# Expert tiles that are full whatever the last block of tokens chooses are listed before that block is routed

## The chip, the cores and the metric

The program runs on one core of one Trainium2 chip. The metric is the device time of one execution in microseconds (us), taken as a median of several runs. A core has five engines with a queue each: TensorE (PE in the profile; PEld is its loading of weights), VectorE (DVE), ScalarE (ACT), GpSimd (POOL) and SyncE (SP), which here issues most transfers (DMA). Instructions of an engine go in the order of its queue and wait on semaphores for what other engines make. All numbers are 32-bit floats.

## The reference

An image of 256 channels and 64 x 64 places passes four layers. Layers 0 and 1 are convolutions and layer 2 is an attention with a mixture of experts (hidden width 256); they come before the change. Layer 3, where the change lies, works on 4096 tokens of 256 channels:

```python
t = t + _L3_attn_ref(_ln_t(t), ...)      # one head: softmax(Q K^T / 16) V over all 4096 tokens
t = t + _L3_ffn_ref(_ln_t(t), ...)       # eight experts, two for each token

gate_logits = xf @ Wg + bg
top_w, top_i = jax.lax.top_k(gate_logits, 2)
top_w = jax.nn.softmax(top_w, axis=-1)
for e in range(8):
    h = jax.nn.gelu(xf @ W1[e] + b1[e])              # 256 -> 1024
    out = out + w_dense[:, e:e + 1] * (h @ W2[e] + b2[e])   # 1024 -> 256
```

So each token goes to two of eight experts, and which two is known only when its attention is done, normalized and multiplied by Wg.

## The kernel before

**Attention** (attn3, L2385 to L2668). The tokens stand in SBUF as `t`, 32 tiles of 128 rows. Queries are taken in eight blocks of 512 (NBLK = 8, NB = 512), and for each block the keys in 16 pairs of tiles (NPAIR = 16). One step of the loop is `scores(g)` for one pair (L2541), `values(g - 2)` for the pair two before (L2575) and `fetch(g + 3)`, which loads keys (L2514). At the end of a block VectorE puts the four accumulators together into oT (L2535 to L2537). In the pairs of the next block come `finish` (L2595), one per tile of the finished block: a product of oT with the value weights (recorded in the helper L148), a division and an addition into `t`, and then `route`, a generator of five steps: statistics and norm; two turns (transposes, L2061) through PSUM; logits, the two best experts, their weights and counts (`top`, `exp`, `weigh`, `count`); and last `place`, `find` and `scatter`, which puts each row of the block by eight indirect DMAs of POOL (L2113) into `xs`, a DRAM array with room of 4096 rows for each expert. A row carries its number, its two weights and its first expert beside its 256 channels (CX = 260). A step of the route is taken every second pair. PE's and POOL's instructions stand in written order in this loop (`tc.manual_schedule`); a scheduler orders the other engines.

At the start of attention, `add(b)` (L2434) adds the results of layer 2's experts to `t`: two loads of `ys`, one issued by SP and one by ACT (L2332), into one of two buffers `room`, which `route` uses too, and two additions (L2440).

After the last block, finish and route of that block follow at once, with nothing else to do for PE, and then **tile_table** (L2121): from the counts per expert it makes a table of 39 tiles of 256 rows (NTILE = 39): expert and first row of each (`tab`), and for the last rows of an expert which are in use (`in`, `off`). Then attention's pools are released.

**Experts** (experts L2173, expert_tiles L2190). 36 tiles always run (MOST = 36), three more only if the table uses them. A tile: `load` reads the expert and the row out of the table into registers of SP and issues loads of x (256 rows), w1 and w2; `turn` transposes x by four PE instructions and a copy by VectorE into xT (L2222); `first` is 32 products into f_h_ps with eight gelus of ACT (L2232); `where` works out on VectorE to which rows of `ys` the results go; `sides` makes sums of weights on POOL (wt, L2259); `second` is 56 products into f_ya_ps and f_yb_ps, additions on VectorE, scaling on ACT (L2301) and two indirect DMAs of POOL (L2302). The loads run two tiles ahead, from three buffers of w1 and w2; the loop (L2314) puts `first(i)` and `turn(i + 1)` ahead of `second(i - 1)`. A scheduler sets the order on the engines here. At last the results are added to `t` and stored (limits3 L2670, store L1361).

Of the kernel before, what the change touches and what calls it, by code (L numbers as in the profile page):

```python
# [19 lines left out]
P = 128  # L20
C = 256
# [28 lines left out]
NI = MT // P  # L50

# [37 lines left out]
class Net:  # L89
# [2031 lines left out]
    def tile_table(self, S, wp, bank):  # L2121


        nc = self.nc
        tl = lambda shape, tag, dt=F32: wp.tile([P] + shape, dt, tag="f_" + tag, name="f_" + tag, bufs=1)
# [8 lines left out]
        nc.vector.tensor_copy(cnt, ci)  # L2134
        ends = tl([NE], "ends")
# [4 lines left out]
        tau = tl([NTILE], "tau")  # L2140
        nc.vector.tensor_scalar(tau, self.count, last, None, ALU.min)
        past = tl([NTILE, NE], "past")
        nc.vector.tensor_tensor(past, bc(ends, 1, NTILE), bc(tau, 2, NE), ALU.is_le)
        ex = S["ex"]
        nc.vector.tensor_reduce(ex, past, AX.X, ALU.add)
        tab = S["tab"]
        nc.vector.tensor_scalar_mul(tab[:, 0, :], ex, float(P))
        nc.vector.tensor_tensor(past, past, bc(cnt, 1, NTILE), ALU.mult)
        skip = tl([NTILE], "skip")
        nc.vector.tensor_reduce(skip, past, AX.X, ALU.add)  # L2150
        nc.vector.tensor_sub(tau, tau, skip)
        nc.vector.tensor_scalar_mul(tau, tau, float(MT))
# [6 lines left out]
        nc.vector.tensor_tensor(past, bc(ex, 2, NE), bc(self.count[:, :NE], 1, NTILE), ALU.is_equal)  # L2159
        nc.vector.tensor_tensor(past, past, bc(rows, 1, NTILE), ALU.mult)  # L2160
        nc.vector.tensor_reduce(skip, past, AX.X, ALU.add)
        nc.vector.tensor_sub(skip, skip, tau)
        nc.vector.tensor_scalar(tau, self.count, last, None, ALU.is_le)
        nc.vector.tensor_mul(skip, skip, tau)

        nc.vector.tensor_tensor(S["in"], bc(self.nth[:, :NI], 1, NTILE), bc(skip, 2, NI), ALU.is_lt)
        nc.vector.tensor_scalar(S["off"], S["in"], -1.0, 1.0, ALU.mult, ALU.add)
        for i in range(0, NTILE, 4):
            n = min(4, NTILE - i)
            part = S["off"][:, i : i + n, :].rearrange("p i k -> p (i k)")  # L2170
            nc.vector.scalar_tensor_tensor(part, self.nth[:, : n * NI], float(2 * N), part, ALU.add, ALU.mult)

    def experts(self, S):  # L2173

        tc = self.tc

        def some(tiles):
            with (
                tc.tile_pool(name=f"f{S['L']}e", bufs=5 if S["L"] == 2 else 3) as wp,
                tc.tile_pool(name=f"f{S['L']}e_ps", bufs=1, space=PSUM) as ps,  # L2180
            ):
                self.expert_tiles(S, tiles, wp, ps)

        some(range(MOST))
        used = self.nc.values_load(S["used"][0:1, 0:1], min_val=0, max_val=NTILE,
                                   skip_runtime_bounds_check_because="worked out from counts of tokens")
        with tc.If(used > MOST):
            some(range(MOST, NTILE))

    def expert_tiles(self, S, tiles, wp, ps):  # L2190
        nc, A = self.nc, self.A
        L, tab = S["L"], S["tab"]
        hidden = 256 if L == 2 else 1024
        KH = hidden // P
        ahead = 3 if L == 2 else 2
        why = "worked out from counts of tokens"

        def load(i):
            e = nc.values_load(tab[0:1, 0, i : i + 1], engines=[mybir.EngineType.SP], min_val=0, max_val=(NE - 1) * P,
                               skip_runtime_bounds_check_because=why)  # L2200
            row = nc.values_load(tab[0:1, 1, i : i + 1], engines=[mybir.EngineType.SP], min_val=0, max_val=NE * N - MT,
                                 skip_runtime_bounds_check_because=why)
            x = wp.tile([P, NI, CX], F32, tag="x", name="f_x", bufs=ahead + 3)
            rows = lambda: nc.sync.dma_start(out=x, in_=self.xs[bass.ds(row, MT), :].rearrange("(i p) c -> p i c", p=P))

            if i > 0:
                rows()
            w1 = wp.tile([P, 2 * hidden + KH], F32, tag="w1", name="f_w1")
            nc.sync.dma_start(out=w1, in_=A[f"f{L}_w1"][bass.ds(e, P), :])
            w2 = wp.tile([P, KH * C + C], F32, tag="w2", name="f_w2")  # L2210
            nc.sync.dma_start(out=w2, in_=A[f"f{L}_w2"][bass.ds(e, P), :])
            if i == 0:
                rows()
            return x, w1, w2

        def turn(x):
            p = ps.tile([P, 2, MT], F32, tag="x", name="f_x_ps", bufs=2)
            for k in range(2):
                for i in range(NI):
                    nc.tensor.transpose(p[:, k, i * P : (i + 1) * P], x[:, i, k * P : (k + 1) * P], self.ident)  # L2220
            xT = wp.tile([P, 2, MT], F32, tag="xT", name="f_xT")
            nc.vector.tensor_copy(xT, p)  # L2222
            return xT

        def first(xT, w1):
            h = wp.tile([P, KH, MT], F32, tag="h", name="f_h")
            for m in range(KH):
                if m % 2 == 0:
                    p = ps.tile([P, 2, MT], F32, tag="h", name="f_h_ps", bufs=3)
                q = p[:, m % 2, :]  # L2230
                self.mm(q, [(w1[:, kt * hidden + m * P : kt * hidden + (m + 1) * P], xT[:, kt, :]) for kt in range(2)])
                nc.scalar.activation(h[:, m, :], q, AF.Gelu, bias=w1[:, 2 * hidden + m : 2 * hidden + m + 1])  # L2232
            return h

        def where(i, x):
# [3 lines left out]
            op = nc.vector  # L2239
            op.tensor_scalar(first, x[:, :, C + 3], S["ex"][:, i : i + 1], None, ALU.is_equal)  # L2240
# [4 lines left out]
            op.tensor_tensor(to, to, S["in"][:, i, :], ALU.mult)  # L2245
            op.tensor_tensor(at, to, S["off"][:, i, :], ALU.add)
# [60 lines left out]
        tiles = list(tiles)  # L2307
# [3 lines left out]
        xT = turn(ld[tiles[0]][0])  # L2311
        to = where(tiles[0], ld[tiles[0]][0])
        done = None
        for i in tiles:  # L2314
# [3 lines left out]
            h = first(xT, w1)  # L2318
            now = (i, h, w2, sides(w2)) + to
            if i < tiles[-1]:  # L2320
                xT = turn(ld[i + 1][0])
                to = where(i + 1, ld[i + 1][0])
            if done is not None:
                second(*done)
            done = now
        second(*done)

    def outputs(self, b, y):

        src = self.ys[: 2 * N, :].rearrange("(r b p i) c -> b p r (i c)", r=2, b=NBLK, i=TPB)  # L2330
        for r in range(2):
            (self.nc.sync, self.nc.scalar)[r].dma_start(out=y[:, r].rearrange("p i c -> p (i c)"), in_=src[b][:, r])  # L2332
# [10 lines left out]
    def moe_state(self, pool, L=2):  # L2343
        tl = lambda shape, tag, dt=F32: pool.tile([P] + shape, dt, tag=tag, name="f_" + tag)
        return {
            "L": L, "to": tl([2, NT], "to", I32), "tab": tl([2, NTILE], "tab", I32), "used": tl([1], "used", I32),
            "big": tl([2, 2, NT // 2], "big"), "r": tl([NT], "r"), "ex": tl([NTILE], "ex"), "in": tl([NTILE, NI], "in"), "off": tl([NTILE, NI], "off"),
# [37 lines left out]
    def attn3(self, t, S):  # L2385
# [6 lines left out]
        with (  # L2392
            tc.tile_pool(name="a3", bufs=1) as pool,
            tc.tile_pool(name="a3d", bufs=1, space=DRAM) as dpool,
        ):

# [8 lines left out]
            wvp = pool.tile([P, 2, C + 1], F32, tag="wvp", name="a3_wvp")  # L2405
# [12 lines left out]
            with (  # L2418
                tc.tile_pool(name="a3w", bufs=2) as wp,
# [224 lines left out]
                with tc.manual_schedule(engines={ET.PE, ET.Pool}):  # L2644
# [15 lines left out]
                    for _ in steps:  # L2660
                        pass
# [262 lines left out]
```

## Time and profile before

| what | value |
|---|---|
| median of 3 runs | 3424.92 us (3424.81 to 3425.16) |
| the profiled execution | 3476.99 us |
| its span (first to last instruction) | 3475.3 us |
| PE busy | 3129.0 us, 90% of the span |
| VectorE busy | 2302.7 us, 66% |
| POOL busy | 1457.9 us, 42% |
| ACT busy | 1332.0 us, 38% |
| moved by DMA | 407 MB, 117 GB/s on average |

The profiled execution is 52 us slower than the runs that are timed without a profile; durations and places below are those of the profiled one. "L2222" is a line of the kernel before; a product of any part may be recorded in the helper at L148, and is told by the names of its tiles (f_h_ps <- f_xT, f_w). A clock of 1.00 is PE's full speed. Places in time are us from the start of the span: layer 3's attention goes from about 1975 to 2880, its experts from about 2926 to 3426, the stores to 3475.

### The profile page before, as it was taken

What the parts mean: (1) busy time and instruction counts of PE and PEld (TensorE: products, weight loads), DVE (VectorE), ACT (ScalarE), POOL (GpSimd) and SP (SyncE); (2) the same over time, 40 slices, a digit from 0 to 9 for tenths busy, and PEclk for the clock granted to TensorE, in tenths of its full rate; (3) what the DMA queues carried; (4) which work ended last, traced back from release to release, by engine and by line L of the source; (5) the groups of instructions that cost most, each with busy time, mean ns of one, the idle gap of its engine ahead of it and who ended that gap; (6) DMA issues with size and microseconds to landing.
All of it is one profiled execution on the core that took longest, in us unless ns stands there. A gap on an engine that the chain in (4) does not pass through costs nothing.

```text
span 3475.3 us, 66162 instructions
## 1 busy us (share of the span) xinstructions
PE 3129.0 (90%) x25772; PEld 2335.4 (67%) x25772; DVE 2302.7 (66%) x5315; ACT 1332.0 (38%) x2550; POOL 1457.9 (42%) x1316
## 2 busy tenths in 40 slices
PE   6779999999977998898959789999999996999997
PEld 3433444344446888666747567888888885999886
DVE  8885777577754777796545576777777775555552
ACT  4444344434325665343423353222222222333331
POOL 2028788788824555333334343000000003555552
PEclk9889999999988999997869899999999997999999
DMA  2145656421143222100138653323333223555554
GB/s 74 40 120 136 169 158 167 119 59 52 48 139 86 74 74 73 35 1 14 46 133 269 210 215 115 94 89 99 99 100 98 82 77 129 209 204 192 203 203 182
DMA packets 241689, 407.01 MB, mean 117 GB/s; under 512 B 78354, under 2 KB 152851, under 8 KB 231891
## 3 DMA queue, kind: packets, MB, share of 16 engines
q1 hardware_dynamic: 212002, 344.40, 31.8%
q0 software_dynamic: 13056, 35.93, 2.7%
q10 hardware_dynamic: 16304, 22.31, 1.9%
q8 instruction: 207, 3.39, 0.4%
q14 instruction: 120, 0.98, 0.1%
HBM read 287.07 MB, written 111.30 MB: 115 GB/s over the span
## 4 chain that ended last, share of the span: by engine, by line
PE 43%; DVE 8%; DMA 5%; issue 5%; POOL 3%; ACT 3%; another core or an unknown queue 0%; SPq 0%; POOLq 0%; DVEq 0%; ACTq 0%
PE a_sa_ps L2547 6%; PE f_h_ps L148 5%; DMA ys<-f_y,f_at 3%; PE a_oa_ps L2586 3%; PE a_ob_ps L2586 3%; PE a_oc_ps L2586 3%; PE l_acc_ps L1156 3%; PE a_sb_ps L2547 3%; PE f_ya_ps L148 2%; PE f_yb_ps L148 2%; POOL ys L2302 2%; DVE l_pr L1152 1%; PE a_od_ps L2586 1%; PE a_sc_ps L2547 1%; PE a_q_ps L148 1%
## 5 line engine op out<-in xcount | busy, mean ns | idle before, releaser
L772 ACT COPY l_sc<-l_s 128x384 f32<-128x384 f32 (+1 forms) x632 | 304.7, 534 | 454.4 <-PE l_s L765 448.4
L777 DVE TENSOR_TENSOR l_sm<-l_s,mask 128x256 f32<-128x256 f32 (+2 forms) x628 | 307.7, 549 | 90.6 <-PE l_s L765 89.5
L2113 POOL DMA_INDIRECT xs<-f_room,f_to x64 | 64.2, 1004 | 701.8 <-issue 588.1
L148 PE MATMUL f_h_ps<-f_xT,f_w 128*128 128x256 f32 x1440 | 341.1, 388 | 18.5 <-DVE f_xT L2222 8.0
L148 PEld LDWEIGHTS f_h_ps<-f_xT,f_w 128*128 128x128 f32 x1440 | 261.9, 192 | 83.6 <-ACT f_h L2232 20.1
L765 PE MATMUL l_s<-l_q,l_k 32*128 32x256 f32 (+3 forms) x2944 | 270.6, 452 | 0.0
L2566 ACT ACTIVATE a_e<-a_e 128x512 f32<-128x512 f32 x256 | 156.1, 631 | 248.6 <-DVE a_e L2536 233.9
L782 POOL TENSOR_TENSOR l_sm<-l_sc,mask 128x768 f32<-128x768 f32 (+1 forms) x116 | 202.4, 1752 | 87.8 <-ACT l_sc L772 87.7
L2232 ACT ACTIVATE f_h<-f_h_ps,f_w 128x256 f32<-128x256 f32 x360 | 167.0, 472 | 187.1 <-PE f_h_ps L148 183.4
L1152 DVE TENSOR_TENSOR l_pr<-l_vk,l_w_ps 128x1280 f32<-128x1280 f32 x128 | 186.5, 1481 | 54.2 <-PE l_acc_ps L1156 36.0
L765 PEld LDWEIGHTS l_s<-l_q,l_k 32*128 32x128 f32 x2944 | 132.4, 183 | 115.2 <-issue 67.5
L2302 POOL DMA_INDIRECT ys<-f_y,f_at x144 | 146.2, 1015 | 138.4 <-ACT f_y L2301 107.8
L1156 PE MATMUL l_acc_ps<-ident,l_pr 128*128 128x128 f32 x1600 | 198.4, 278 | 6.2 <-POOL l_pr L1147 6.2
L1156 PEld LDWEIGHTS l_acc_ps<-ident,l_pr 128*128 128x128 f32 x1600 | 185.0, 144 | 12.7 <-POOL l_pr L1147 7.6
L786 POOL TENSOR_TENSOR l_sm<-l_sc,mask 128x256 f32<-128x256 f32 (+1 forms) x220 | 184.8, 867 | 15.3 <-ACT l_sc L772 14.5
L2259 POOL TENSOR_TENSOR f_wt<-f_w 128x512 f32<-128x512 f32 x72 | 89.8, 1266 | 218.2 <-PE f_ya_ps L148 206.6
L2547 PE MATMUL a_sa_ps<-a_q,a_kt 128*128 128x256 f32 x512 | 156.8, 388 | 17.4 <-DVE a_u L2552 16.6
L2551 ACT COPY a_u<-a_sa_ps 128x256 f32<-128x256 f32 x128 | 47.7, 372 | 292.6 <-PE a_sa_ps L2547 288.4
L811 PE MATMUL l_b_ps<-l_sm,l_v 128*32 128x256 f32 (+2 forms) x2176 | 153.5, 372 | 0.0
L2547 PE MATMUL a_sa_ps<-a_qt,a_kt 128*128 128x256 f32 x512 | 153.2, 381 | 0.0
L782 POOL TENSOR_TENSOR l_sm<-l_sc,mask_c 128x768 f32<-128x768 f32 (+1 forms) x64 | 122.3, 1928 | 39.4 <-ACT l_sc L772 39.0
L2547 PE MATMUL a_sb_ps<-a_qt,a_kt 128*128 128x256 f32 x512 | 132.3, 381 | 0.0
(558 smaller groups left out, 7319.7 us busy)
## 6 DMA issues: line engine op xcount, KB each, us to landing
a_kt<-a_kd SPq DMA_DIRECT2D x128, 512.0 KB
f_w<-in_f_w SPq DMA_DIRECT2D x36, 1152.0 KB
f_w<-in_f_w SPq DMA_DIRECT2D x36, 1028.0 KB
xs<-zero SPq DMA_DIRECT2D x8, 4160.0 KB
l_vk<-vt SPq DMA_DIRECT2D x180, 128.0 KB
f_x<-xs SPq DMA_DIRECT2D x72, 260.0 KB
f_w<-in_f_w SPq DMA_DIRECT2D x36, 384.0 KB
l_rcp<-l_recd SPq DMA_DIRECT2D x48, 256.0 KB
```

What stands on the lines that cost most here:

```text
L148: self.nc.tensor.matmul(out, lhsT, rhs, start=(i == 0), stop=(i == len(pairs) - 1))
L765: nc.tensor.matmul(s[pair, j][:, at : at + m, :], key(hp), qs[hp], start=(z == 0), stop=(z == len(pieces) - 1))
L772: nc.scalar.copy(sc[:, j], s[1, j])
L777: nc.vector.tensor_tensor(to(pair, j, kind, at), pick(s[pair, j], kind, which), mask, ALU.mult)
L782: nc.gpsimd.tensor_tensor(out[:, :, at, :], of[:, :, which, :], bc(mask, 1, 2), ALU.mult)
L786: nc.gpsimd.tensor_tensor(to(1, j, kind, at), pick(sc[:, j], kind, which), mask, ALU.mult)
L1152: nc.vector.tensor_tensor(pr, vk, bc(held["w"][:, j, dy], 3, D), ALU.mult)
L1156: nc.tensor.matmul(acc[:, m, j, :], pf[:, dx, m * P : (m + 1) * P], self.ident, is_transpose=True, start=(j == 0 and dy == 0 and dx == 0 a ...
L2232: nc.scalar.activation(h[:, m, :], q, AF.Gelu, bias=w1[:, 2 * hidden + m : 2 * hidden + m + 1])
L2302: nc.gpsimd.indirect_dma_start(out=self.ys_parts[(i % 4) * NI + k], in_=y[:, k, :], in_offset=None, out_offset=bass.IndirectOffsetOnAxis(a ...
L2547: mm = lambda out, i, right: nc.tensor.matmul(out, A[i], right, start=True, stop=True)
L2586: nc.tensor.matmul(out, vs[:, j, i, :], right, start=(j == 0 and side != 1), stop=(j == NPAIR - 1 and side != 0))
```

## The change

The sum of what an expert holds after seven blocks of tokens can only grow. Tiles of 256 rows that are full then stay full: at least (2 x 3584 - 8 x 255) / 256, rounded down, which is 20 (FULL). The change makes two tables: A with these 20 tiles, made before the last block of attention is over, and B with the others, made from all counts.

- `full_table` (new) makes table A in pair 9 of the last block, after the route of the seventh block, which in the last block goes one step per pair and not every second. All rows of its tiles are in use: `in` and `off` are constants. `gone` keeps how many tiles of each expert are in A.
- Right after it tile 0 is loaded: x, and w1 and w2 into buffers lent by attention (the tags "w1" and "w2" in the pool `k3`, which stays open into the experts; in attention they hold `ks`, and y of `add` for blocks 2 and later). In pair 14 tile 0 is turned (four transposes, one copy).
- Attention's other pools are released once the loop is over. The last block's `finish` and route are no longer part of attention: `finish(0)` comes ahead of tile 0's first product, the other three between its pairs of products, the five steps of the route and then tile_table (for B) after the first and second halves of tiles 0 to 3. PE's instructions have a written order until then, and the scheduler's afterwards.
- w1 and w2 have two buffers and the lent one (tiles 0, 3, 6 and so on), `f_x_ps` has one PSUM bank instead of two, because a bank stays with finish and route. `room` has one buffer instead of two. `add` of blocks 0 and 1 uses the buffers of e and et.
- In layer 2 the experts keep one table of 39; xT and h have three buffers instead of five there.

```diff
+FULL = (2 * (N - NB) - NE * (MT - 1)) // MT
...
+    def full_table(self, S, wp, bank):
+        T, n = S["A"], FULL
+        c_ps = bank()[:, :NE]
+        self.mm(c_ps, [(self.all_one, S["cum"])])
+        ...
+        nc.vector.tensor_single_scalar(ci, ci, MT.bit_length() - 1, ALU.arith_shift_right)
+        nc.vector.tensor_copy(full, ci)
+        nc.vector.tensor_tensor_scan(ends, self.one.to_broadcast([P, NE]), full, 0.0, ALU.mult, ALU.add)
+        ...
+        nc.vector.tensor_copy(T["tab"][:, 1, :], tau)
+        gone = S["gone"]
+        nc.vector.tensor_sub(gone, full, ends)
+        nc.vector.tensor_scalar(gone, gone, float(n), 0.0, ALU.add, ALU.max)
+        nc.vector.tensor_tensor(gone, gone, full, ALU.min)
+        nc.gpsimd.memset(T["in"], 1.0)
+        nc.gpsimd.memset(T["off"], 0.0)
...
     def tile_table(self, S, wp, bank, early=False):
+        if early:
+            nc.vector.tensor_sub(cnt, cnt, S["gone"])
...
     def first(xT, w1, between=None):
+            for m in range(0, KH, 2):
+                ...
+                    products(m, p)
+                    products(m + 1, p)
+                    gelu(m, p)
+                    gelu(m + 1, p)
+                    for f in between[m // 2 : m // 2 + 1]:
+                        f()
...
+        def step():
+            if steps:
+                steps.pop(0)()
+                if not steps:
+                    written.close()
...
+            if pre and i == 0:
+                return pre["tile"]
+            lent = pre and i % 3 == 0
...
-            p = ps.tile([P, 2, MT], F32, tag="x", name="f_x_ps", bufs=2)
+            p = ps.tile([P, 2, MT], F32, tag="x", name="f_x_ps", bufs=1 if early else 2)
...
         for i in tiles:
             if i + ahead <= tiles[-1]:
                 ld[i + ahead] = load(i + ahead)
             x, w1, w2 = ld.pop(i)
-            h = first(xT, w1)
+            h = first(xT, w1, (pre["ahead"][1:] if i == 0 else ()) if steps else None)
             now = (i, h, w2, sides(w2)) + to
+            step()
             if i < tiles[-1]:
                 xT = turn(ld[i + 1][0])
                 to = where(i + 1, ld[i + 1][0])
             if done is not None:
                 second(*done)
+                step()
...
-                            elif j % 2 == 0:
+                            elif j % 2 == 0 or b == NBLK - 1:
                                 next(steps, None)
-                    for _ in steps:
-                        pass
-                    banks += ["sa", "sb", "sc"]
-                    for i in range(TPB):
-                        finish(NBLK - 1, i)
-                    for _ in route((NBLK - 1) * TPB, TPB):
-                        pass
-                with tc.manual_schedule(engines={ET.PE, ET.Pool, ET.DVE}):
-                    self.tile_table(S, wp, bank)
+                            if b == NBLK - 1 and j == TPB + 5:
+                                self.full_table(S, keep, bank)
+                                ...
+                                tile = self.expert_load(S, S["A"]["tab"], 0, ..., True)
+                            if b == NBLK - 1 and j == NPAIR - 2:
+                                xT = self.expert_turn(tile[0], bank().rearrange("p (k n) -> p k n", k=2), one([2, MT], "xT"))
+            left.close()
+            last = route((NBLK - 1) * TPB, TPB)
+            go = lambda: next(last, None)
+            self.experts(
+                S, [go] * 5 + [lambda: self.tile_table(S, keep, bank, True)],
+                {"pool": keep, "tile": tile, "xT": xT, "ahead": [lambda i=i: finish(NBLK - 1, i) for i in range(TPB)]},
+            )
```

## The prediction

> **What bounds the kernel now.** I read the page's busy times first, then the windows (the time as a table of stretches), then the chain of work that ended last, then the waits of the one stretch that stood out. Times are those of the profiled execution.
>
> ```profile
> PE 3129.0 (90%) x25772; PEld 2335.4 (67%) x25772; DVE 2302.7 (66%) x5315; ACT 1332.0 (38%) x2550; POOL 1457.9 (42%) x1316
> ```
>
> TensorE is busy 90% of the span. The windows (columns: stretch, its us, busy us of PE, PEld, DVE, ACT and POOL, granted clock, DMA share, GB/s) say where the other 10% lies at the end of the kernel:
>
> ```profile
> 2750.00:2800.00 50.00, 49.88 (x241) 43.65 (x240) 38.09 (x101) 13.00 (x26) 8.04 (x9) 1.00 0.31 97
> ...
> 2885.00:2896.00 11.00, 5.93 (x24) 4.95 (x24) 5.62 (x29) 1.71 (x3) 2.18 (x4) 0.60 0.10 36
> 2896.00:2911.00 15.00, 1.53 (x6) 1.43 (x6) 8.64 (x47) 0.67 (x2) 7.94 (x8) 0.50 0.20 71
> 2911.00:2925.00 14.00, 1.94 (x8) 1.57 (x8) 4.70 (x11) 1.49 (x2) 4.97 (x4) 0.50 0.90 359
> 2925.00:2945.00 20.00, 19.25 (x87) 16.40 (x88) 12.27 (x37) 7.62 (x16) 4.98 (x4) 0.84 0.50 191
> 2950.00:3400.00 450.00, 445.14 (x2979) 405.45 (x2978) 247.32 (x643) 157.43 (x362) 247.26 (x197) 1.00 0.55 200
> ```
>
> Attention (49.88 of 50) and the experts (445 of 450) are bound by PE at full clock. Between them PE works 9.4 us of 40 and its clock falls to half. The chain of work that ended last, at that place:
>
> ```profile
> 2880.11 0.71 PE a_q_ps L148 x2
> ...
> 2887.80 11.47 issue
> ...
> 2908.37 2.43 DMA xs<-f_room,f_to
> ...
> 2913.49 6.71 DMA f_x<-xs
> ...
> 2925.75 16.92 PE f_h_ps L148 x64
> ...
> 2977.34 6.93 PE f_h_ps L148 x32
> ```
>
> The last block is finished, routed and scattered (eight scatters, 2899.3 to 2909.3), the table is made, the rows come back, and only then do expert products begin. The waits in 2870 to 2945 (total us, times, longest):
>
> ```profile
> PE f_x_ps L2220 <- DMA f_x<-xs: 22.4, 1, 22.4
> ...
> PE f_h_ps L148 <- DVE f_xT L2222: 3.8, 1, 3.8
> ```
>
> **What the Trainium skill says.** "TensorE: Matmul & The Clock Gate", Part 1, says that after an idle window of about 3.4 us PE falls to half clock, and needs a busy window to come back. The trace agrees: 0.50 from 2886.8 to 2931.2, the return 5.5 us after work resumed. "SBUF — State Buffer", Who interferes with whom, says that VectorE and GpSimd share a port pair and that one blocks the other for a whole instruction. The trace agrees: L2241, L2242 and L2248 took 1.19, 1.18 and 1.23 us beside POOL's L2259 (1.27 us), 0.15 to 0.17 us otherwise. "ScalarE: Activation LUTs", What ACT_TABLE_LOAD costs, gives 1.28 us for a load; the trace shows 1.28 too.
>
> **The change, part by part.** I sum from 2880.1 (the last oT) to the first product of the fifth tile, because from there both kernels run the same steady tiles (13.61 us: f_h 6.93, turn 0.43, second products 6.27). Before, that product starts at 2977.34, so the stretch is 97.2 us.
>
> *Removed.* With 20 tiles listed from seven blocks, tile 0 needs nothing of the last block. What PE has to do in the stretch: finish 3.44 (L148, 2 + 14 products and the gaps), four first halves 4 x 6.93 = 27.7, four turns 1.7, three second halves 3 x 6.27 = 18.8, the last block's routing 3.0 (its turn 0.5, logits 1.85 at full clock as in 2761.0, place 0.6, counts 0.1). Sum 54.7. If nothing waits, the gain is 97.2 - 54.7 = 42.5 us. It contains 3.8 us that before lost on its first tiles (64 products took 16.92 for 2 x 6.93, the rest half clock).
>
> *Added in attention's last block.* The list of full tiles (some 20 small VectorE operations), tile 0's load (SP's queue, behind all key loads), four transposes (0.43) and the counts product (0.1) enter. Routing of block 6 goes one step per pair instead of every second. A pair is 6.5 us; the fullest then holds about 9.0 us of VectorE, and the pairs around it 4.7 (35.7 of 50). The excess of 2.5 is mostly eaten by three score buffers: I take 1.1 us lost, 0 to 2.5. With the 0.5 of PE work, 1.6. Tile 0's rows wait for block 6's eight scatters, which end about 15 us ahead of the transposes: nothing, hidden by five pairs of attention.
>
> *Lent buffers.* Blocks 2 to 7's additions take their y from one buffer instead of two. In the trace the six additions are 16 us apart (2002 to 2084), and a pair of y loads needs about 5.5 us (1 MB at 359 GB/s, plus the 2.4 us that a landing took): covered. ACT now issues block 2's y ahead of those of blocks 0 and 1, at the start where all wait: 1 us, from -1 to 2. One of the two PSUM banks of f_x goes to finish and routing: see the next step.
>
> *The written order of the first four tiles.* Tile 1's rows can be asked for only when oT is done (2880.1), landing at about 2883; weights at about 2888. PE reaches its products after finish, first(0) and turn(1): 2880.1 + 3.4 + 6.9 + 0.4 = 2890.9. It then needs xT(1) from VectorE. VectorE's order ahead of that copy is where(0), four finishes (0.65 each, each one released by PE through one shared bank), where(1), hs, the limits, six operations of where(2), several of them at 1.2 us beside POOL's L2259. I put the copy's end between 2892 and 2897 and take 2894.6: stall 3.7 us (1 to 6). Before, such a copy had a second half to hide it; for tile 1 there is none, and PE's queue being in order, everything behind it waits. A hole of that size is at the edge of an idle window: half clock afterwards, 2 us (0 to 4).
>
> *ACT.* The exponentials and the square root of the last block's routing come among the gelus: two table loads at 1.28 and eight exponentials; 0.7 us on PE (0 to 2).
>
> *The fifth tile on.* x(5) comes behind the last block's eight scatters in program order. These stand on POOL behind ys(1): they end about 17.5 us after second(1) (7.4 + 8 x 1.26), land 2.4 later, and the rows 2.7 later: 22.6 us after second(1), while PE asks for them after 21.3. Stall 1.7 (0 to 5). VectorE's early table (about 8 us) makes one tile hold 16 us of VectorE against 13.6; later tiles have 7.5 and absorb it: nothing, 1 us if ys fall behind.
>
> *Unchanged.* 36 tiles run in both; 20 + 16. The last tiles, stores and limits are the same.
>
> Sum: -42.5 + 1.6 + 1.0 + 3.7 + 2.0 + 0.7 + 1.7 = -31.8 us. The profiled span goes from 3475.3 to 3443.5, the profiled execution from 3476.99 to about 3445.2. The median of the runs before is 3424.92, 52 us (1.5%) below the profiled time; the stretch is on the path in both, so I subtract it whole: **3393 us**, ratio 0.991. A difference of 0.2%, 6.8 us, is about what a measurement can tell from none.
>
> **The rivals.** *All hidden.* xT(1) is copied before PE gets there, the clock stays up, x(5) comes in time: the gain is 38 to 42 us, 3383 to 3387. For it: VectorE is busy only 12.27 of 20 us in 2925 to 2945. Against: no second half covers tile 1.
>
> *The stalls are larger.* The copy of xT(1) ends at 2897 or later, PE runs at half clock for 5.5 us and more (as before), the shared bank makes finish go at VectorE's pace, and x(5) is 5 us late: 6 + 4 + 4 + 5 + 2 + 1.6 = 23 lost, with 1 to 6 more if the routing, written between products, meets late VectorE answers (each of its five steps waits for a chain such as top's 3.7 us). Gain 10 to 25, 3400 to 3415. For it: the 22 operations of top and 1.2 us operations beside POOL.
>
> *No early start.* The experts' buffers come free only when attention's are released by the last scatters; tile 1 and all others then start as before. Gain 0 to 7 (only tile 0's 7 us), 3418 to 3425. Against: tile 1's rows wait for oT alone, as the instructions' waits show, not for the scatters.
>
> *Slower.* The lent buffer decides. Each y load of blocks 2 to 7 must wait for the addition before it, and its issue stands in ACT's queue behind the work of a pair; if a load lands L us later than VectorE, whose order is written, wants it, scores and with them PE wait L, six times. It decides from 6 L = 32, L = 5.3 us, that is when a load lands over 21 us after the addition before it. At L = 8 the time is 3393 + 48 = 3441. For it: ACT's queue is in order, and one wait of VectorE for y is there already (4.3 us). Against: 5.5 us needed, 16 there.
>
> **How the numbers follow.** Central case (gain 26 to 37, 3388 to 3399) 0.48; all hidden 0.17; larger stalls 0.23; no early start 0.05; slower 0.07. The range 3383 to 3412 leaves out the last two and the ends. The likeliest alone: 3388 to 3399. Faster by over 0.2%: 0.48 + 0.17 + 0.23 = 0.88. Within: 0.05. Slower: 0.07.
>
> **What would show it.** Right: the wait of 22.4 us on f_x is gone, expert products begin by about 2884 and follow finish; a stall of some us before the second tile's first product, released by f_xT; the fifth tile's first product near 2945 (less what attention changes); the last scatters near the third or fourth tile; one more small wait on f_x for tile 5. Wrong: a PE clock of 0.50 for over 6 us after 2890; waits of PE on routing's VectorE steps in the written order; waits of DVE on y in 2000 to 2090; f_x of tile 0 waited for inside attention.

## The result

| | median us | ratio to the kernel before |
|---|---|---|
| before | 3424.81 | 1 |
| the changed kernel | 3404.69 (3396.68 to 3407.44) | 0.9941 (0.9925 to 0.9956) |

The change gains 20.1 us (before is the median of five runs here; the 3424.92 from which the prediction started was that of three). Forecast were 31.8 us (3393); the time lies in the range given (3383 to 3412), outside the likeliest case's own range (3388 to 3399), and in the place of the rival with larger stalls (3400 to 3415).

The profiled execution of the changed kernel took 3404.69 us, span 3402.8. The profiled execution of before, 3476.99 us, was 52 us longer than the runs without a profile. Layer 2's routing, which is the same code in both kernels, took 156 us from first to last scatter there against 108 in the profile after, which would be 48 of them. It comes back below in kernels with and without the change, so the two traces are compared part by part and not span against span. Lines have moved: 148 is now 152, 2216 to 2232 (turn, first) are now 2241 to 2303, 2240 to 2248 (where) are 2325 to 2333, 2301 and 2302 are 2386 and 2387, 2113 is 2117, 2602 is 2708.

The engines in the whole span, from the page of the changed kernel:

```profile
PE 3095.0 (91%) x25774; PEld 2314.3 (68%) x25774; DVE 2299.0 (68%) x5331; ACT 1329.1 (39%) x2552; POOL 1460.9 (43%) x1318
```

The windows of the end (columns as before: stretch, its us, PE, PEld, DVE, ACT, POOL, clock, DMA share, GB/s). The last oT ends at 2830.6:

```profile
2850.00:2865.00 15.00, 15.00 (x104) 14.07 (x103) 8.66 (x24) 4.63 (x12) 4.09 (x3) 1.00 0.10 42
...
2880.00:2895.00 15.00, 15.00 (x101) 13.80 (x100) 7.54 (x22) 6.79 (x15) 12.02 (x12) 1.00 0.43 155
2895.00:2910.00 15.00, 5.08 (x17) 3.88 (x16) 6.84 (x38) 2.47 (x6) 7.51 (x7) 0.70 0.54 177
2910.00:2930.00 20.00, 20.00 (x144) 18.68 (x143) 10.89 (x32) 5.30 (x12) 7.68 (x6) 0.97 0.59 220
```

The gap of 40 us that stood between attention and experts is gone: but for two waits of 2.0 and 2.2 us just behind the last oT, PE works through. But a new hole has opened at 2895 to 2910, of which PE fills 5 us. The waits of 2826 to 2930 (total us, times, longest) name its parts:

```profile
DVE f_first L2325 <- DMA f_x<-xs: 10.2, 1, 10.2
...
PE f_h_ps L152 <- ACT f_h L2303: 12.1, 2, 9.9
...
PE a_q_ps L152 <- DVE t L2708: 2.0, 1, 2.0
```

And the chain of work that ended last puts them in order:

```profile
2894.61 2.44 DMA xs<-f_room,f_to
...
2897.30 2.77 DMA f_x<-xs
...
2900.09 0.59 DVE f_first L2325
...
2904.55 0.61 DVE f_y L2379
...
2905.18 0.91 ACT f_y L2386 x2
2906.08 0.73 ACT f_h L2303 x2
...
2906.86 3.78 PE f_h_ps L152 x8
```

This is to be read from its end. PE waits 9.9 us in the middle of tile 4's first products for a gelu (ACT). ACT is not busy: the gelu stands in its queue behind the scaling of tile 2's results (L2386), which waits for tile 2's addition on VectorE (L2379). VectorE stands idle for most of that time too: the addition stands in its queue behind the first operation of tile 5's `where` (L2325), which waits for tile 5's rows, and these were asked for only when the last block's eight scatters had landed. (From the rows' landing to that addition, 2900.1 to 2904.5, VectorE works off what had piled up behind the wait: operations of the table, of the `where` and of tile 2's results.) Three queues pass one wait on. Then PE goes on at half clock (3.78 us for eight products, which are listed with 1.89 in tile 0).

To compare kernels whatever their start, the next table reads from the timelines when the first product of some tiles begins, in us after the end of the last oT, and when the last tile's last product into f_h_ps begins ("last"):

| kernel | tile 4 | tile 5 | tile 8 | last |
|---|---|---|---|---|
| before | 97.1 | 110.7 | 152.3 | 532.8 |
| changed | 61.0 | 87.0 | 129.9 | 509.5 |
| changed, again | 62.0 | 88.2 | 129.8 | 509.4 |

By tile 4 the change has gained 36 us, by tile 5 24 us, at the end 23.3 us.

### The profile page after: what moved, and what is told of

It reads as the page before. It is cut to its first block, busy times and chain, and to the rows that moved or that the text cites. A ratio compares the mean times of both kernels' runs of the same rounds, so it can differ in the third digit from the quotient of the medians.

```text
span 3402.8 us, 66193 instructions
## 1 busy us (share of the span) xinstructions
PE 3095.0 (91%) x25774; PEld 2314.3 (68%) x25774; DVE 2299.0 (68%) x5331; ACT 1329.1 (39%) x2552; POOL 1460.9 (43%) x1318
## 4 chain that ended last, share of the span: by engine, by line
PE 41%; DVE 8%; DMA 5%; issue 4%; ACT 3%; POOL 3%; SPq 0%; POOLq 0%; DVEq 0%; ACTq 0%
PE a_sa_ps L2653 6%; PE f_h_ps L152 6%; PE a_oa_ps L2692 3%; PE a_ob_ps L2692 3%; DMA ys<-f_y,f_at 3%; PE a_oc_ps L2692 3%; PE a_sb_ps L2653 3%; PE f_ya_ps L152 3%; PE l_acc_ps L1160 2%; PE f_yb_ps L152 2%; POOL ys L2387 2%; PE a_od_ps L2692 1%; PE a_q_ps L152 1%; PE a_sc_ps L2653 1%; PE a_qkv_ps L152 1%
## 5 line engine op out<-in xcount | busy, mean ns | idle before, releaser
L2692 PE MATMUL a_ob_ps<-a_et,a_vs 128*128 128x256 f32 x512 | 132.2, 381 | 0.0
```

What stands on the lines that cost most here:

```text
L2692: nc.tensor.matmul(out, vs[:, j, i, :], right, start=(j == 0 and side != 1), stop=(j == NPAIR - 1 and side != 0))
```

## The experiments

Ratios are to runs of the kernel before on the same chip, with 95% intervals. The theory (called the queue theory in the expectations): VectorE's `where` of tile 5, placed by the scheduler ahead of tile 2's addition and waiting for rows, costs 12 us. Rivals: VectorE or GpSimd are overloaded there; PE's written order makes the waits; the late rows cost by themselves.

**The changed kernel again.**

> The changed kernel again, as the measure of the other three runs on the same chip. Both theories: ratio to the kernel before 0.993 to 0.996; in its trace one PE wait of about 10 us in tile 4's first products and a half clock behind it.

Measured: 3407.38 us, 0.9954 (0.9939 to 0.9970), 17.4 us under the kernel before on that chip. Its trace has the same wait (tile 5 at 88.2).

**Tile 5's rows earlier.** They are asked for in tile 2, ahead of the last route step and so of the scatters.

```diff
             if i + ahead <= tiles[-1]:
                 ld[i + ahead] = load(i + ahead)
+                if pre and i == 2:
+                    sooner[5] = self.expert_rows(of(5, "tab"), order[5][1], wp.tile(...))
```

> Only the rows of the sixth tile (tile 5) are asked for one route step earlier in the program, ahead of the last block's scatters instead of behind them. Queue theory (VectorE's queue holds tile 5's where, which waits for these rows, ahead of the additions of y of tile 2; ACT's scaling and gelus and so PE stand behind it): the 10 us wait and the half clock after it vanish, about 12 us less than the changed kernel, ratio to before about 0.9905. Rival (VectorE is simply overloaded by route and table in these tiles, some 16 us of work in 13.6): the wait stays at 5 us or more, at most 5 us less, ratio 0.9925 or above.

Measured: 3398.81 us, 0.9923 (0.9907 to 0.9939): 8.6 us under the changed kernel by the medians, between what the theory (0.9905) and the rival (0.9925 or above) were to give. In its profiled execution tile 5 begins at 75.8 instead of 88.2, the whole 12.4 us. But there tile 6 then begins at 96.7, where 13.6 more would be 89.4, and the end (507.2) is only 2.2 us sooner. The profiled execution was the slowest of the six (3406.40 us), so that the trace doesn't show where the rest of the 8.6 us comes from. PE, VectorE and POOL at that place, from the timeline:

```profile
2919.68 4.81 PE L152 MATMUL f_h_ps<-f_xT,f_w 128*128 128x256 f32 x12 [5.14 <-ACT f_h L2314]
...
2910.08 4.42 DVE L2343 TENSOR_TENSOR f_first<-f_first,f_x 128x2 f32<-128x2 f32 x1
...
2910.75 2.50 POOL L2355 TENSOR_TENSOR f_wt<-f_w 128x512 f32<-128x512 f32 x2
2913.20 2.62 POOL L2355 TENSOR_TENSOR f_wt<-f_w,f_wt 128x512 f32<-128x512 f32 x2
```

The same chain one tile later, with another wait at its head: an operation of `where` on 128 x 2 numbers, 0.15 us otherwise, is listed with 4.42 us while POOL, late after its eight scatters, does two tiles' sums close together. The addition of tile 3 stands behind it, then ACT, then PE for 5.1 us, then half clock. So the queue theory holds for the wait it was made for. The rival may have its part next in line: that GpSimd's burst made the 4.42 us is read from the two standing side by side, and no run took the burst away alone.

**VectorE's order.** The rows come as late as in the changed kernel, but from tile 3's turn to tile 4's end VectorE's order is written, with tile 5's `where` behind the additions.

```diff
+            if pre and i == 3:
+                dve.enter_context(self.tc.manual_schedule(engines={mybir.EngineType.DVE}))
             if i < tiles[-1]:
                 xT = turn(ld[i + 1][0])
-                to = where(i + 1, ld[i + 1][0])
+                if not (pre and i == 4):
+                    to = where(i + 1, ld[i + 1][0])
             if done is not None:
                 second(*done)
                 step()
+            if pre and i == 4:
+                to = where(5, ld[5][0])
             done = now
+            if pre and i == 4:
+                dve.close()
```

> The rows of tile 5 come as late as in the changed kernel; only VectorE's order is written from tile 3's turn to tile 4's end, with tile 5's where behind the additions of tiles 2 and 3. Queue theory: the 10 us wait in tile 4's first products vanishes; what is left is PE's own wait for tile 5's rows at its transposes, 1 to 3 us, so about 8 to 10 us less than the changed kernel, ratio 0.9910 to 0.9918. If the late landing itself costs PE the time (through the transposes), the wait only moves there and stays at 7 us or more: ratio 0.993 to 0.994. Overload rival: no change of more than 3 us.

Measured: 3399.24 us, 0.9931 (0.9915 to 0.9947), 8.1 us under the changed kernel by the medians. The 9.9 us wait is gone with the rows as late as ever; what is left of them is PE's own wait at the transposes, and half clock behind it:

```profile
2903.16 0.72 PE L2241 MATMUL f_x_ps<-ident,f_x 128*128 128x128 f32 x4 [3.49 <-DMA f_x<-xs]
...
2904.10 1.91 PE L152 MATMUL f_h_ps<-f_xT,f_w 128*128 128x256 f32 x4
...
2912.40 4.50 PE L152 MATMUL f_h_ps<-f_xT,f_w 128*128 128x256 f32 x20
```

The four products at 2904.10 are the last of tile 4's 32, and tile 5 begins at 2912.40, 81.4 us after the last oT (88.2 in the changed kernel on this chip). From the end of tile 3's first products (2886.60) to there PE has 20.3 us of work, by the parts that the prediction sums, and takes 25.8. So lateness itself costs some 5.5 us here, 3.5 of wait and about 2 of half clock, and the order in VectorE's queue made the other 7 of the 12.4. Lateness has a larger part than the theory gave it (1 to 3 us), and the ratio lies at the edge of the case in which the wait only moves (0.993 to 0.994). Tile 8 begins at 125.1, the end is at 504.7, 4.7 us sooner than in the changed kernel.

**Tile 0's where in attention.** It was meant to clear VectorE between the last oT and the first finish.

```diff
                                 xT = self.expert_turn(tile[0], ...)
+                                to = self.expert_where(tile[0], S["A"], 0, ...)
```

> Only tile 0's where (nine small VectorE operations) is done in attention, behind tile 0's transposes, instead of between the last oT and the first finish. Theory: PE's wait of 2.0 us for the first finish's division and addition goes, and with it the half clock over the next eight products (1.7 us): 2 to 4 us less than the changed kernel, ratio 0.9930 on the 0.9941 of it. Rival (the one shared bank and POOL's sums are enough to hold finish up): the wait stays at over 1 us and the time is the same within 1 us.

Measured: 3413.02 us, 0.9968 (0.9957 to 0.9980): 5.6 us slower than the changed kernel, not faster. The waits of attention's last pairs:

```profile
DVE f_first L2248 <- DMA f_x<-xs: 6.5, 1, 6.5
...
PE a_sa_ps L2656 <- DVE a_e L2646: 4.5, 1, 4.5
```

In the program this `where` stands behind the transposes of pair 14. The scheduler put it some pairs sooner, as we take it because it reckoned tile 0's rows to be there; they came later, VectorE stood for 6.5 us, and with it scores and PE for 4.5, with half clock behind. From the first score to the last oT this kernel takes 884.3 us, the changed one 876.3. It is the same fault in another place, made by accident. What the experiment was for did not come about: PE's wait of 2.0 us for the first finish is gone, but waits of 1.3 and 3.9 us follow, and tile 1 begins at 16.1 as it does in the changed kernel (16.2).

**Without PE's written order.**

```diff
-                if pre:
+                if False:
                     order.enter_context(tc.manual_schedule(engines={mybir.EngineType.PE}))
```

> The changed kernel without the written order of PE in the first four tiles; the scheduler places PE's instructions there too. Queue theory (the loss sits in VectorE's order, which the scheduler makes in both): the wait of about 10 us in tile 4 stays, time within 4 us of the changed kernel, ratio 0.9935 to 0.9965. Rival (PE's written order is what makes the stalls): the waits of PE in tiles 0, 1 and 4 shrink by 5 us or more, ratio 0.9925 or below.

Measured: 3401.76 us, 0.9933 (0.9919 to 0.9948). Tile 4, 5, 8 and the end at 61.2, 87.9, 129.5 and 509.2, as in the changed kernel, with a PE wait of 9.89 us for ACT in tile 4. PE's written order neither makes the waits nor is it needed for the gain.

**The route in one piece.** The lists and tile 0's early load stay; finish, route and table come ahead of tile 0's first product. (Shown in part: PE's order stays written up to tile 3.)

```diff
-                S, [go] * 5 + [lambda: self.tile_table(S, keep, bank, True)],
-                {"pool": keep, "tile": tile, "xT": xT, "ahead": [lambda i=i: finish(NBLK - 1, i) for i in range(TPB)]},
+                S, [],
+                {"pool": keep, "tile": tile, "xT": xT, "ahead": [lambda i=i: finish(NBLK - 1, i) for i in range(TPB)] + [go] * 5
+                 + [lambda: self.tile_table(S, keep, bank, True)]},
```

> Half of the change: the lists, tile 0's early load and turn and the loads of tile 1 stay, but finish, the five steps of the last block's route and the table come all at once ahead of tile 0's first product, as before the change, and PE's order is written so. It tells the gain of listing ahead (no wait for the rows) from the gain of laying the route between the experts' products. Theory: PE reaches tile 0's first product about 17 us after the last oT, at half clock, and tile 4's about 70 us after it (97.2 before, 61.0 in the changed kernel); with no wait for tile 5's rows the rest runs steadily, so it ends about as early as the changed kernel: 3398 to 3404 us, ratio 0.992 to 0.995. If laying between is what gains, it is 10 us or more slower than the changed kernel, ratio over 0.997.

Measured: 3432.51 us, 1.0021 (1.0010 to 1.0033), slower than before the change. Tile 0 begins 28.6 us after the last oT and not 17, tile 4 at 99.3:

```profile
2831.49 2.05 PE L152 MATMUL a_q_ps<-a_wvp,a_oT 128*128 128x257 f32 x4 [3.71 <-DVE t L2710]
...
2843.09 1.35 PE L2065 MATMUL a_q_ps<-ident,f_room 128*128 128x128 f32 x4 [3.71 <-DVE f_room L240]
...
2853.71 0.60 PE L152 MATMUL a_q_ps<-f_both,before 128*128 128x32 f32 x2 [3.06 <-DVE f_both L2090]
```

With nothing between its steps each of them is waited for, through one bank and at half clock: 28 us before tile 0's first product, which begins at 0.6 in the changed kernel. Laid between that kernel's products, the same steps leave PE full in 2850 to 2895. What listing ahead is worth alone, this run doesn't tell. Tile 0 begins 17.1 us sooner than in the kernel before (28.6 against 45.7), but from there to tile 4 are 70.7 us with 48.2 of PE work in them, by the prediction's parts, and much of the difference is this experiment's own. Without products to lay between, tiles 0 to 2 take their first products singly, and a dozen waits for a gelu, of 0.56 us mostly, make 6.7 us. And tile 2's rows, now asked for behind the scatters, come late: VectorE has tile 2's `where` ahead of tile 1's copy, and PE waits for the copy.

```profile
2871.55 0.23 DVE L2325 TENSOR_SCALAR f_first<-f_x,f_exA 128x2 f32<-128x2 f32 x1 [5.89 <-DMA f_x<-xs]
...
2874.22 2.08 PE L152 MATMUL f_h_ps<-f_xT,f_w 128*128 128x256 f32 x4 [5.08 <-DVE f_xT L2242]
```

It is the fault of tile 5 once more, at tile 1. Most of the rest is half clock. How the gain is shared between listing ahead and laying between stays open.

**VectorE's order written throughout**, with tile 5's rows early and the table two tiles later; and the same with POOL's order written and the scatters in two halves. (Shown in part: tile 1's turn also comes ahead of tile 0's `where`, and the `where` of tiles 5 and 6 behind the additions.)

```diff
+            dve.enter_context(self.tc.manual_schedule(engines={mybir.EngineType.DVE}))
             for f in pre["ahead"][:1]:
                 f()
...
-                S, [go] * 5 + [lambda: self.tile_table(S, keep, bank, True)],
+                S, [go] * 5 + [lambda: None] * 6 + [lambda: self.tile_table(S, keep, bank, True)],
```

> A mended version: tile 5's rows asked for ahead of the scatters; VectorE's order written from the last oT to tile 5's end, with each where of tiles 0, 5 and 6 behind the additions that PE waits for through ACT and the norm behind tile 1's copy; the table made two tiles later. Queue theory: the waits in tile 0 (2.0), tile 1 (2 to 3.4) and tiles 4 and 5 (7 to 12 with half clock) go, so tile 8's first product comes about 115 to 118 us after the last oT (129.9 in the changed kernel): 3389 to 3396 us, ratio 0.989 to 0.992. If GpSimd's burst (eight scatters and two tiles of sums, some 18 us in 13.6) is what costs, a wait of 5 us or more stays in tile 5 or 6: ratio 0.9925 or above.

> The mended version with GpSimd's order written too and the last block's eight scatters in two halves, four ahead of tile 3's sums and four behind them. If GpSimd's burst costs, this is faster than the one with VectorE's order alone by 3 to 6 us; if only VectorE's order did, it is the same within 2 us.

Measured: 3408.74 us, 0.9955 (0.9943 to 0.9967) and 3407.46 us, 0.9951 (0.9937 to 0.9965): nothing gained on the changed kernel (tile 8 at 130.9 and 130.2, where 115 to 118 were expected), and the two are the same. Tile 5 does come at 81.5, but the gain is lost at other places:

```profile
2874.28 4.57 PE L152 MATMUL f_ya_ps<-f_wt,f_hs 128*128 128x128 f32 x24 [4.28 <-DVE f_hs L2362]
...
2949.42 2.93 PE L152 MATMUL f_h_ps<-f_xT,f_w 128*128 128x256 f32 x6 [6.43 <-ACT f_h L2314]
```

In program order the sums that a second half needs (f_hs) stand behind the whole choice of experts, ahead of which VectorE waits 5.0 us for the logits. And where the written order ends, the scheduler's begins again: tile 8's `where` waits 3.1 us for its rows, and the wait of 6.43 follows. That halving the scatters did not help does not clear POOL, since neither run was free of the other waits.

**All rows two tiles sooner.** If a `where` that waits for rows is the trouble, rows that come early should end it.

```diff
+                for k in {1: (4, 5), 2: (6,)}.get(i, (i + 4,)) if pre and 1 <= i and i + 4 <= tiles[-1] else ():
+                    sooner[k] = self.expert_rows(of(k, "tab"), order[k][1], wp.tile(..., bufs=7))
```

> The changed kernel with all rows asked for two tiles sooner (seven buffers of x instead of five; tiles 5 and 6 ahead of the scatters), nothing else. Queue theory (a where that waits for rows holds up the additions behind it, and so ACT and PE): the wait of 10 us in tile 4 goes, and no wait of VectorE on f_x over 1 us is left after tile 1; tile 8's first product comes 112 to 120 us after the last oT (129.8 in the changed kernel), time 3390 to 3398 us, ratio 0.989 to 0.9925. Rival (GpSimd's and VectorE's added work costs what is lost, rows or no rows): waits of 7 us or more with f_x in time, ratio 0.9935 or above.

> The same, and the second table made two tiles later, in tile 6, away from the scatters. If VectorE's load in tiles 3 and 4 costs (table about 8 us there), 2 to 5 us faster than the one without; else the same within 2 us.

Measured: 3533.95 us, 1.0213 (1.0198 to 1.0227) and 3539.98 us, 1.0227 (1.0213 to 1.0241): some 3% over the kernel before, 100 us from what the queue theory gave. The rival's ratio (0.9935 or above) is met, but not by its cause, as the next run shows. (In the second the table also comes two tiles later.) A tile now takes about 17 us. The waits of 150 us in the middle of the experts:

```profile
DVE f_at L2342 <- DMA ys<-f_y,f_at: 62.1, 9, 7.7
...
PE f_h_ps L152 <- ACT f_h L2314: 21.1, 8, 3.2
```

VectorE waits for no rows any more. It waits in nearly every tile, up to 7.7 us, to write `at`, the row numbers that a `where` makes, into one of four buffers, because the scatter of ys that reads the numbers four tiles back has not landed. In VectorE's queue each `where` now stands sooner than in the changed kernel: its `at` is ahead of sums for the second half (f_hs) and of the copy into xT, where it came behind both. That the scheduler did so because it reckons the rows to be there is our inference. Again ACT and PE stand behind. (In the changed kernel the waits for `at` come to 37.4 us from 2926 to 3400, in before to 37.7 from 2976 to 3426, and PE's waits for ACT there to 5.2 and 4.4.) And tile 4 takes 24.0 us here too, though no row is late. The table's place made no difference that this could show.

**Ten buffers for what a where makes.** If so, buffers alone must mend it.

```diff
-            tl = lambda tag, dt=F32: wp.tile([P, NI], dt, tag=tag, name="f_" + tag, bufs=4)
+            tl = lambda tag, dt=F32: wp.tile([P, NI], dt, tag=tag, name="f_" + tag, bufs=10 if pre else 4)
```

> The kernel with all rows two tiles sooner, which ran at 17.2 us a tile (1.021 of before) with 62 us of waits of VectorE in 150 us for earlier results to land before it may write a where's row numbers, and now ten buffers for what a where makes, instead of four; nothing else. Queue theory (any wait of a where stands ahead of additions that ACT and PE need, whatever it waits for): those waits go, tiles take 13.6 us again, tile 8's first product comes 112 to 125 us after the last oT (129.8 in the changed kernel, 136.8 with four buffers), and the last one 492 to 504 us after it (509.4 and 602.1): ratio to before 0.988 to 0.994. Rival (the earlier rows cost by their transfers or their place in SyncE's queue): tiles stay at 16 us or more, ratio over 1.015.

Measured: 3434.84 us on a chip where the kernel before took 3463.48 us: 0.9914 (0.9899 to 0.9929). Six more buffers of 8 bytes per partition for each of five small tiles took about 100 us off the run before it. Tile 8 begins at 125.3, the last first products at 499.7, 9.8 us sooner than in the changed kernel. The windows of 150 us in the middle, first of this kernel, then of the one with four buffers:

```profile
3123.00:3273.00 150.00, 150.00 (x1015) 137.75 (x1014) 82.83 (x221) 53.26 (x122) 84.66 (x67) 1.00 0.56 204
```

```profile
3150.00:3300.00 150.00, 126.53 (x819) 112.98 (x817) 79.75 (x169) 38.89 (x93) 69.95 (x52) 0.98 0.44 161
```

PE has no idle time left there. But tile 4 still takes 22.0 us (tile 5 at 84.5; waits of 1.8 and 3.1 us in front of products and half clock behind); ACT, in front of the gelu that the second of them waits for, stands 3.7 us for a cause that the trace doesn't show. So only some 2.5 of the 9.8 us are won at tile 5, some 2 more by tile 8, and 5.2 in the steady tiles, whose small waits are gone (13.6 us a tile against 13.8). By the ratios this version is ahead of the changed kernel (0.9914 against 0.9941 and 0.9954), but the two were not run on one chip, and its interval touches that of the first.

**The kernel before again**, for its layer 2.

> The kernel before, for a second profile of it. If the 48 us by which its first profile was longer between layer 2's first and last scatter (156 us against 108 in the changed kernel) belong to that one execution, this one shows 108 there, and tile 4's first product again 97 us after the last oT.

Measured: 3470.52 us in one execution; tile 4's first product at 96.5, as expected. But layer 2's scatters took 148 us again, so the first profile was no single accident: on this chip and that of the ten buffers, the three kernels with all rows early show 147 to 148 too, and before takes 3461 and 3463 us and not 3425. What makes those 40 us is not known. It lies in code that all kernels share, and ratios on one chip are free of it.

## Why the prediction was right and where it was wrong

- **To tile 4's first product: right, by its own sum.** Forecast were 54.7 of work plus 3.7 (tile 1's copy), 2.0 (half clock) and 0.7 (ACT), 61.1 us; measured 61.0. That it fits so closely is luck, since the parts came out otherwise: 2.0 at the first finish, which was not forecast (where(0) stood beside POOL's sums; with it in attention the wait was gone), half clock over the next eight products (3.3 instead of 1.7), and 2.2 at tile 1, where the copy (ending 2847.35) and the gelus behind two table loads of ACT (2843.10 and 2845.26, 1.28 us each; the prediction counted two in all, the trace has four by tile 3) were late together.
- **"The fifth tile on": the step that failed.** The lateness was foreseen: 22.6 us after second(1)'s end were forecast, and tile 5's rows were there at 2900.1, 22.8 us after it (2877.3). The wait was priced where PE itself needs the rows, at its transposes: 1.7 us, at most 5 (its own figures, 22.6 and 21.3, give 1.3). What the runs showed in its place is a term of 12.4 us (9.9 wait, 2.05 and 0.4 of half clock), because the rows are first needed by VectorE, for a `where`, which stands ahead of an addition that ACT and then PE wait for. With the order of VectorE mended the wait at the transposes is 3.5 us, within what was forecast, and half clock adds about 2. The prediction named what stands in VectorE's queue for tile 1's copy, and did not ask the same for tile 5. The trace of before already had the chain in small, in its fourth tile, where a `where` waits for a scatter of ys and PE, behind addition and gelu, for 0.48 us:

```profile
2962.48 0.95 DVE L2246 TENSOR_TENSOR f_at<-f_to,f_off 128x2 int32<-128x2 f32 x1 [2.25 <-DMA ys<-f_y,f_at]
```

```profile
2967.79 2.86 PE L148 MATMUL f_h_ps<-f_xT,f_w 128*128 128x256 f32 x12 [0.48 <-ACT f_h L2232]
```

- **The other terms.** Attention's last block was to lose 1.6 us and lost none (from the first score to the last oT 878.5 and 877.0 us in the two profiles of before, 877.1 and 876.3 after). Its start was to lose 1.0 and lost 1.9: from layer 2's last scatter of results to the first transposes 15.4 became 16.5, from there to the first score 14.2 became 15.0. In layer 2's experts nothing was forecast. From layer 2's last scatter of rows to its last of results were 178.3 and 179.7 us in the two profiles of before and 176.0 to 181.2 in those after, which doesn't settle whether the fewer buffers of xT and h cost 1 or 2 us.
- **The sum.** From the last oT on, 42.5 - 3.7 - 2.0 - 0.7 - 1.7 = 34.4 were forecast; with 12.4 for 1.7 it is 23.7, and 23.3 were measured. With 1.4 gained in attention (by the first profiles; the second ones give 0.7) and 1.9 lost at its start that leaves 22.8, against 20.1 by the medians; the last 3 us are within what single profiles and layer 2's experts vary by, and are not accounted for.
- **Tile 0 inside attention.** Block 6's scatters were to end about 15 us ahead of its transposes and ended 16 ahead (2810.1; the rows were asked for at 2811.8, and the transposes at 2826.1 did not wait). The rival with a lent buffer that decides did not come about (VectorE waits for no y in 2000 to 2090), and "no early start" is refuted by tile 0's first product at 0.6 us.
- **The rival "larger stalls"** had the size right and the place wrong: the route's steps, laid between products, cost PE nothing that the trace shows after tile 1.

## What to carry to other kernels

When a transfer becomes late, look for the first instruction on any engine that waits for it, not for the one that was meant to need it, and then for what stands behind that instruction on its engine and who waits for that. A scheduler that orders an engine's queue before the run can put a small operation that will wait ahead of work that is ready; the cure is not always to bring the input sooner, since another wait (here a buffer four tiles deep) may take its place. A chain of short dependent steps is worth laying between products even where it takes little of any engine's time.

## What was not expected of the hardware

- A VectorE operation on 128 x 2 numbers was listed with 4.42 us (0.15 us otherwise) while GpSimd issued a scatter and did sums of about 1.25 us each one after the other; the prediction had reckoned with 1.2 us, one sum's time.
- PE fell to half clock after an idle time of 2.0 us (2833.1 to 2835.1), and in the second profile of the same kernel the same wait left the clock up. First the one, then the other:

```profile
2835.09 1.11 PE L152 MATMUL a_q_ps<-a_wvp,a_oT 128*128 128x257 f32 x4 [1.99 <-DVE t L2708]
2836.04 3.48 PE L152 MATMUL f_h_ps<-f_xT,f_w 128*128 128x256 f32 x8
```

```profile
2834.49 1.11 PE L152 MATMUL a_q_ps<-a_wvp,a_oT 128*128 128x257 f32 x4 [1.99 <-DVE t L2708]
2835.44 1.89 PE L152 MATMUL f_h_ps<-f_xT,f_w 128*128 128x256 f32 x8
```

The Trainium skill, "TensorE: Matmul & The Clock Gate", Part 1, speaks of an idle window of about 3.4 us that runs on its own. The traces' records of the granted clock show such windows, but they need not be idle throughout. In the changed kernel the stretches at half clock in the places told of here are 3.41 and 10.24 us long, one and three times 3.41. Count the time at full clock back from each fall in pieces of 3.41 us: from layer 3's attention on, in all fourteen traces, PE was idle for 1.73 us or more in the last piece before each of 119 falls, and for 1.99 us or less in each of 5712 other pieces. So idle time of little more than half a piece brought the clock down. The wait of 2.0 us above lay within one piece (2832.77 to 2836.18) and the clock fell at its end; in the second profile a border of two pieces (2833.78) fell into it. A wait of 2.2 us at tile 1 of the first profile, parted into 1.2 and 1.0, left the clock up too. (In the kernel before the record has the half clock from 2887.2 to 2931.5, thirteen pieces, where the prediction read 2886.8 to 2931.2.)
